# Where the tables of the third and fourth slot and the scale of the second matrix stand in a gated cross-attention kernel

## The chip, the cores and the metric

The kernel runs on one core of a Trainium2 chip. The metric is the device time of one execution in microseconds (us). The engines are TensorE (PE in the profile, with its weight loads as PEld), VectorE (DVE), ScalarE (ACT), GpSimd (POOL) and SyncE (SP). Each works through its own instructions in a fixed order and waits on semaphores for the others.

## The reference

There are 16 sequences, each with 224 tokens of width 512 and a context of 750 rows of width 384, part of them masked. Cut to what matters:

```python
# attention block
q = layernorm(x) @ W_q ; k = context @ W_k ; v = context @ W_v       # 8 heads of 64
attn = softmax(where(mask, q @ k.T / 8, -max))
x = x + tanh(g_xattn) * ((attn @ v) @ W_o + b_o)
# feed-forward block: 512 -> 2048 -> 512, activations and weights quantised
def weight_quant(w):                       # a matrix of -1, 0, 1 times one scale
    scale = 1 / clip(mean(abs(w)), 1e-5)
    return clip(round(w * scale), -1, 1) / scale
h = gelu(act_quant(rmsnorm(layernorm(x))) @ weight_quant(w1).T + b1)
x = x + tanh(g_ffn) * (act_quant(rmsnorm(h)) @ weight_quant(w2).T + b2)
```

The scale of a weight matrix needs the mean over the whole matrix, so no element of it can be rounded before all of it has been summed.

## The kernel before

**Slots.** The mask keeps few context rows of each sequence, so only kept rows are loaded. The sequences are sorted by their number of kept rows; sequence number s of that order is "slot s". Slots 0 to 7 hold up to 192 rows, slots 8 to 15 up to 128. The work of a slot s has these parts, by function of `compact_path`:

- `select(s)` makes the tables. Six VectorE comparisons write `ind` (L830, one buffer for all slots), twelve small matmuls sum it into `pi` (L836), two VectorE instructions turn `pi` into row numbers `keys` (L850), and one writes the mask (L866).
- `gather(s)` (L880) issues two indirect DMAs from GpSimd that fetch the context rows by `keys` into `ctx`, which has two buffers.
- `context_pieces(s)` is a list of pieces: transposes of the context (`ctxp`, L905), keys (`kp`, L916, two pieces) and values (`vp`, L931, and `vr`, L942).
- `query_pieces(s)` transposes normalised tokens (`xnp`, L1014) and makes queries (`qp`, L1035). `norm_pieces(s)` normalises tokens on VectorE and GpSimd (L979 to L988) and fetches later ones (L807).
- `scores(s, n)`, n from 0 to 3, makes a quarter of the slot's scores (`sim`, L1074), takes maxima on VectorE (L1088), exponentials on ScalarE (L1098), the reciprocal of the sums on VectorE (L1107), and scales the probabilities on GpSimd (L1108). `turn_probs` transposes them (`ptp` L1128, `ptr` L1135) and `weighted(s)` multiplies them with the values (`av`, L1151 and L1166).

**Weights.** The two feed-forward matrices are prepared beside slots 0 and 1. `load_weights` brings chunks of [128, 1024] into `raw`, `sum_weights` (L1388 on VectorE, L1392 on ScalarE) sums them, `scale_weights(wi)` (L1398 to L1411) ends in one matmul `wtotp` (L1400) and a few tiny VectorE instructions that make the scale. `round_weights` then needs two VectorE instructions a chunk (L1421 writes integers into `raw`, L1422 clips them into `w16`, which has three buffers), and `turn_weights` transposes a chunk (`wp`, L1441 for the first matrix, L1445 for the second) and evicts it as fp8. There are eight chunks a matrix. A chunk of the second matrix is loaded into the buffer of `raw` that the same chunk of the first has left.

**Order.** Program order is made by `merge`, which interleaves three streams (attention of slot s, `other`: what prepares slot s + 1 and later ones, and `flow`: weights or feed-forward) by the costs written beside the pieces. `weave` mixes the context pieces and the query pieces of the next slot. A scheduler then places the instructions on the engines. Ahead of the loop stands a block under `behind`, with the scores of slot 0, the sums of the first matrix, `scale_weights(0)` and `select(2)`. In the loop, slot s emits `norm_pieces(s + 2)`, `gather(s + 2)`, `select(s + 3)` and then the woven pieces of slot s + 1. In slot 1 `scale_weights(1)` is the first piece of `flow`.

**Pools.** After slot 1 the pool `raw` (eight buffers of 4 KB in a partition) is closed and the pool `rows` (`y`, `hq`, `hqT`, eight buffers of 4 KB) is opened in its place. From then on `residual` fetches tokens into `y` (L807) and adds a bias on GpSimd (L1207); the first three such pairs can be fetched early.

Of the kernel before, what the change touches and what calls it, by code (L numbers as in the profile page):

```python
# [733 lines left out]
def compact_path(ctx, tc, sh, x, context, out, late_loads, stages):  # L734
# [5 lines left out]
    B, S, D = x.shape  # L740
# [82 lines left out]
    def select(s):  # L823

        st = live[s]
        cap = CAPS[s]
        nt = 2 if cap > P else 1
        ind = pa.tile([TJ, NJ, 192], BF16, tag="ind", name=f"ind_{s}", bufs=1)
        for n in range(NJ):
            nc.vector.tensor_scalar(ind[:, n, :cap], sh.place[:TJ, :cap], sh.upto[:, n, s : s + 1], None, ALU.is_ge)  # L830
        load["v"] += 6 * 170
        pi = gen([P, 2], F32, f"pi_{s}")
        for t in range(nt):
            rows = rows_of(s, t)
            for n in range(NJ):
                nc.tensor.matmul(  # L836
                    pi[:rows, t : t + 1],
                    lhsT=ind[:, n, t * P : t * P + rows],
                    rhs=sh.one[:, 0:1],
                    start=(n == 0),  # L840
                    stop=(n == NJ - 1),
                )

        if s > 1:
            keys = pa.tile([P, 2], I32, tag="keys", name=f"keys_{s}", bufs=3)
        else:
            keys = across.tile([P, 2], I32, name=f"keys_{s}")
        for t in range(nt):
            rows = rows_of(s, t)
            nc.vector.tensor_scalar(  # L850
                keys[:rows, t : t + 1],
                pi[:rows, t : t + 1],
                float(J - 1),
                sh.first[:rows, s : s + 1],
                ALU.min,
                ALU.add,
            )
        st["keys"] = keys

        if s > 1:  # L860
            mb = pa.tile([TQ, 320], F32, tag="mask", name=f"mask_{s}", bufs=1)
        else:

            mb = early[:TQ, 2 * RING + 2 * s * S : 2 * RING + 2 * s * S + 320]
        nm = 320 if nt > 1 else P
        nc.vector.tensor_scalar(  # L866
            mb[:, :nm], sh.place_f[:TQ, :nm], sh.slots[:TQ, 0, s : s + 1], -FMAX, ALU.is_ge, ALU.mult
        )
        st["mask"] = mb

    def gather(s):
        st = live[s]
        nt = 2 if CAPS[s] > P else 1
        if s:
            kept = pa.tile([P, 2, C], F32, tag="ctx", name=f"ctx_{s}", bufs=2)
        else:
            kept = early[:, 2 * D : 2 * D + 2 * C].rearrange("p (t c) -> p t c", t=2)
        for t in range(nt):
            rows = rows_of(s, t)
            nc.gpsimd.indirect_dma_start(  # L880
                out=kept[:rows, t, :],
                out_offset=None,
                in_=kctx,
                in_offset=bass.IndirectOffsetOnAxis(ap=st["keys"][:rows, t : t + 1], axis=0),
                bounds_check=B * J - 1,
                oob_is_err=False,
            )
        st["ctx"] = kept
# [137 lines left out]
    def query_pieces(s):  # L1026
        st = live[s]

        def query(p):
            if p == 0:  # L1030
                st["qT"] = pa.tile([P, NP, S], F32, tag="qT", name=f"qT_{s}", bufs=2)
            pq = gen([P, 2, S], F32, f"qp_{s}_{p}")
            for i in range(2):
                for d in range(ND):
                    nc.tensor.matmul(  # L1035
                        pq[:, i, :],
                        lhsT=sh.wq[:, d, (p + i) * P : (p + i + 1) * P],
                        rhs=st["xnT"][:, d, :],
                        start=(d == 0),
                        stop=(d == ND - 1),  # L1040
                    )
            evict(st["qT"][:, p : p + 2, :], pq, 2 * S)

        pieces = [(0.4, lambda t=t: turn(t)) for t in tiles_of(s)]
        pieces += [(3.0, lambda p=p: query(p)) for p in (0, 2)]
        return pieces
# [151 lines left out]
    late = {}  # L1198
# [197 lines left out]
    def scale_weights(wi):  # L1396
        tot = small(f"wtot_{wi}")
        nc.vector.tensor_reduce(tot[:, 0:1], weight_sums[wi], AX.X, ALU.add)  # L1398
        pt = gen([P, 1], F32, f"wtotp_{wi}")
        nc.tensor.matmul(pt, lhsT=sh.ones, rhs=tot[:, 0:1], start=True, stop=True)  # L1400
        mean = small(f"wmean_{wi}")
        nc.vector.tensor_scalar(mean[:, 0:1], pt, 1.0 / (FF * D), 1e-5, ALU.mult, ALU.max)
        sw = pa.tile([P, 1], F32, name=f"sw_{wi}")
        nc.vector.reciprocal(sw, mean[:, 0:1])
        isw = pa.tile([P, 1], F32, name=f"isw_{wi}")
        nc.vector.reciprocal(isw, sw)
        if wi == 0:
            nc.vector.tensor_scalar(isw, isw, 1.0 / 127.0, None, ALU.mult)
        else:

            nc.vector.tensor_scalar(isw, isw, sh.tgates[:, 1:2], 1.0 / 127.0, ALU.mult, ALU.mult)  # L1411
        weight_scale[wi] = sw
        sh.isw[wi] = isw
# [35 lines left out]
    def weight_pieces(wi):  # L1449

        p = []
        if wi == 1:
            p += [(0.0, lambda: scale_weights(1))]
        for c in range(NPC + 2):
            if c < NPC:
                p += [(0.2, lambda c=c: round_behind(wi, c))]
                if wi == 0:
                    p += [(0.0, lambda c=c: load_weights(1, c))]
            if c > 1:
                p += [(0.6, lambda c=c: turn_weights(wi, c - 2))]  # L1460
                if wi == 0:
                    p += [(0.0, lambda c=c: sum_weights(1, c - 2))]
        return p
# [18 lines left out]
    def weave(a, b):  # L1482

        outl = []
        ia = ib = 0
        while ia < len(a) or ib < len(b):
            if ib >= len(b) or (ia < len(a) and ia * len(b) <= ib * len(a)):
                outl.append(a[ia])
                ia += 1
            else:  # L1490
                outl.append(b[ib])
                ib += 1
        return outl
# [30 lines left out]
    with ExitStack() as behind:  # L1524
        for instruction in latest.values():
            behind.enter_context(tc.issue_after(instruction))
        scores(0, 0)
        scores(0, 1)
        for _, piece in queries[3:] + keys_values[3:]:
            piece()  # L1530
        for c in range(NPC):
            sum_weights(0, c)
        for _, piece in norm_pieces(1):
            piece()
        scores(0, 2)
        scores(0, 3)
        scored = latest["max"]
        scale_weights(0)
        select(2)

        held = [sh.wo[0:1, 0, 0:1], sh.wo[0:1, 2, 0:1], sh.wo[P // 2 : P // 2 + 1, 2, 0:1]]
        for dst in held + [sh.bo[0:1, 0:1], sh.b1[0:1, 0:1], sh.b2[0:1, 0:1]]:
            nc.scalar.copy(dst, weight_sums[0][0:1, NPC - 1 : NPC])
# [4 lines left out]
    projected = raised = lowered = 0  # L1548
    for s in range(B):
        other = norm_pieces(s + 2) if s + 2 < B else []  # L1550
        if s + 2 < B:
            other.append((0.0, lambda s=s: gather(s + 2)))
        if s + 3 < B:
            other.append((0.0, lambda s=s: select(s + 3)))
        if s + 1 < B:
            other += weave(context_pieces(s + 1), query_pieces(s + 1))
        flow = []
        if s < 2:
            flow = weight_pieces(s)
        else:  # L1560
            complete = 256 * (projected + 1) <= S * s
            if projected == 0:
                nc.gpsimd.tensor_scalar(sh.bo, sh.bo, sh.tgates[:, 0:1], None, ALU.mult)
                nc.gpsimd.tensor_scalar(sh.b2, sh.b2, sh.tgates[:, 1:2], None, ALU.mult)
            if complete:
                flow.append((0.0, lambda i=projected: residual(i)))
            if raised < projected:
                flow += up_pieces(raised)
                raised += 1
            if complete:  # L1570
                flow += project_pieces(projected)
                projected += 1
                if lowered < raised:
                    flow += down_pieces(lowered)
                    lowered += 1
        merge(attention_pieces(s), other, flow)
        if s == 1:

            late["stage"].close()
            late["rows"] = ctx.enter_context(tc.tile_pool(name="rows", bufs=1))  # L1580
        if s + 1 < B:
            scores(s + 1, 0)
            scores(s + 1, 1)
# [45 lines left out]
```

## Time and profile before

| | |
|---|---|
| median of 3 runs | 754.19 us (750.54 to 754.37) |
| the profiled execution | 754.13 us |
| its span, first to last instruction | 752.3 us |
| mean granted TensorE clock | 0.969 |
| busy: PE, DVE, ACT, POOL | 680.9, 502.4, 408.2, 396.7 us |
| from 37.4 us to 74.8 us (first scores of slot 0's second half to first scores of slot 1) | TensorE idle 3.38, 1.44 and 0.96 us |
| from 74.8 us to 111.0 us (first scores of slot 1 to those of slot 2) | TensorE idle 2.73 and 1.26 us, and 0.16 us |
| from 111 us to 640 us | TensorE idle 10.7 us in nine waits for the scaled probabilities (L1108, the longest 3.4), at most 1.8 us in any other wait |

The busy time of an engine says how loaded it is, and the idle times with what ended them say where another engine sets the pace. Since the loop has one order on every engine, an instruction that comes late on one engine holds back everything behind it there. The two stretches in the table are the ones that the change reorders.

### The profile page before, as it was taken

Reading aid. Unit: us, or ns where it says so; the run is one execution under the profiler, and the core shown is the slowest. Engines: PE = TensorE matmul, PEld = TensorE weight load, DVE = VectorE, ACT = ScalarE, POOL = GpSimd, SP = SyncE. Lnnn points to the kernel's source line nnn. Section 1 sums busy time; section 2 is a strip of 40 time slices with the busy share of each in tenths; the row PEclk is TensorE's granted clock in tenths of the full one; section 3 lists DMA queues with packets and bytes.
Section 4 is the critical chain, followed back from the end, with each engine's and each line's share of the span. In section 5 each row is a group of like instructions: output and inputs, shape, how many; then the busy total and the mean of one; then the engine's idle time right before and its main releaser. Section 6 shows DMA issues by size and latency. Waiting matters only on the chain.

```text
span 752.3 us, 11360 instructions
## 1 busy us (share of the span) xinstructions
PE 680.9 (91%) x3900; PEld 433.7 (58%) x3900; DVE 502.4 (67%) x1284; ACT 408.2 (54%) x963; POOL 396.7 (53%) x541
## 2 busy tenths in 40 slices
PE   4979799999999999998999999999999999889642
PEld 3867677675656565665655665666666656433221
DVE  5595856866684674755749667497675949495860
ACT  2557645383763836635757368274655656560530
POOL 5593675463654645546356564565654544535141
PEclk9989899999999999999999999999999999999877
DMA  7775031032222322122233313132131222223250
GB/s 240 275 240 177 27 88 31 15 73 57 82 51 60 87 57 71 40 71 68 36 91 75 84 53 62 43 89 62 54 74 54 57 71 57 71 52 54 47 102 31
DMA packets 87218, 58.77 MB, mean 78 GB/s; under 512 B 75488, under 2 KB 75632, under 8 KB 87024
## 3 DMA queue, kind: packets, MB, share of 16 engines
q1 hardware_dynamic: 79024, 32.00, 18.7%
q0 software_dynamic: 8128, 25.96, 11.0%
q8 instruction: 33, 0.54, 0.3%
q14 instruction: 33, 0.27, 0.1%
HBM read 32.26 MB, written 7.34 MB: 53 GB/s over the span
## 4 chain that ended last, share of the span: by engine, by line
PE 50%; DVE 17%; issue 12%; POOL 9%; ACT 5%; DMA 5%; POOLq 0%; ACTq 0%; DVEq 0%; SPq 0%
PE qp L1035 9%; PE op L1214 8%; PE fp L1329 8%; PE hp L1284 6%; PE vp L931 4%; PE kp L916 3%; PE sim L1074 3%; DVE a L1307 3%; PE ptp L1128 2%; PE av L1151 2%; DVE h L1292 2%; ACT p L1098 2%; DVE p L1088 2%; DVE hq L1310 2%; POOL p L1108 2%
## 5 line engine op out<-in xcount | busy, mean ns | idle before, releaser
L1329 PE MATMUL fp<-w2T,hqT 128*128 128x512 fp8e4 x448 | 106.7, 394 | 14.9 <-DMA hqT<-hq 14.9
L1108 POOL TENSOR_TENSOR p<-p,rec 112x768 f32<-112x768 f32 (+1 forms) x64 | 83.5, 1307 | 68.0 <-DVE rec L1107 42.8
L1284 PE MATMUL hp<-w1T,xqT 128*128 128x512 fp8e4 x448 | 107.2, 384 | 8.8 <-DVE h L1292 6.1
L1098 ACT ACTIVATE p<-p,nm 112x192 f32<-112x192 f32 (+1 forms) x256 | 106.4, 418 | 11.8 <-DVE nm L1088 11.6
L1035 PE MATMUL qp<-xnT,wq_sb 128*128 128x224 f32 x512 | 105.2, 359 | 0.6 <-ACT xnT L780 0.6
L1214 PE MATMUL op<-wo_sb,xoT 128*128 128x512 f32 x224 | 103.7, 599 | 0.0
L1035 PEld LDWEIGHTS qp<-xnT,wq_sb 128*128 128x128 f32 x512 | 97.1, 193 | 6.4 <-issue 3.3
L1292 DVE SCALAR_TENSOR_TENSOR h<-hp,c,b_bc 128x1024 f32<-128x1024 f32 x56 | 71.6, 1279 | 40.8 <-PE hp L1284 38.3
L1329 PEld LDWEIGHTS <-hqT 128*128 128x128 bf16 x448 | 44.0, 101 | 73.6 <-DMA hqT<-hq 17.5
L1088 DVE CUSTOM_DVE_ANT_0 p<-sim,mask 112x128 f32<-112x128 f32 (+1 forms) x224 | 57.7, 313 | 33.0 <-PE sim L1074 33.0
L1307 DVE TENSOR_REDUCE a<-h 128x1 f32<-128x2048 f32 x28 | 63.9, 2282 | 22.7 <-ACT h L1304 22.6
L1284 PEld LDWEIGHTS <-xqT 128*128 128x128 bf16 x448 | 43.5, 98 | 58.0 <-issue 16.0
L1333 DVE SCALAR_TENSOR_TENSOR y<-fp,c,y 128x512 f32<-128x512 f32 x28 | 20.9, 745 | 81.0 <-PE fp L1329 81.0
L1335 POOL DMA_INDIRECT out_dram<-y,token x28 | 30.8, 1099 | 80.0 <-DVE y L1333 75.7
L1315 ACT ACTIVATE h<-h 128x2048 f32<-128x2048 f32 x28 | 53.4, 1908 | 21.9 <-DVE hq L1310 14.5
L1304 ACT ACTIVATE h<-h 128x2048 f32<-128x2048 f32 x28 | 53.5, 1909 | 18.3 <-DVE k L1225 11.2
L1214 PEld LDWEIGHTS op<-wo_sb,xoT 128*128 128x128 f32 x224 | 40.6, 190 | 38.9 <-issue 36.4
L916 PE MATMUL kp<-ctxT,wk_sb 128*128 128x192 f32 (+1 forms) x384 | 61.2, 307 | 0.0
L916 PEld LDWEIGHTS kp<-ctxT,wk_sb 128*128 128x128 f32 x384 | 55.7, 194 | 6.2 <-issue 4.3
L1272 POOL TENSOR_TENSOR y<-y,b_bc 128x512 f32<-128x512 f32 x28 | 36.5, 1304 | 39.0 <-DVE fx L1253 38.7
L780 ACT COPY pT<-ptp 128x448 f32<-128x448 f32 x62 | 32.2, 536 | 39.7 <-PE ptp L1128 38.7
L1074 PE MATMUL sim<-kT,qT 64*112 64x192 f32 (+1 forms) x512 | 49.8, 313 | 0.3 <-DVE h L1292 0.2
(173 smaller groups left out, 1182.3 us busy)
## 6 DMA issues: line engine op xcount, KB each, us to landing
raw<-in_L_ffn_w_dram SPq DMA_DIRECT2D x16, 512.0 KB
wq_sb<-in_L_xattn_W_q_dram SPq DMA_DIRECT2D x1, 1024.0 KB
b_bc<-in_L_ffn_b_dram SPq DMA_DIRECT2D x1, 1024.0 KB
wk_sb<-in_L_xattn_W_k_dram SPq DMA_DIRECT2D x1, 768.0 KB
wv_sb<-in_L_xattn_W_v_dram SPq DMA_DIRECT2D x1, 768.0 KB
wo_sb<-in_L_xattn_W_o_dram SPq DMA_DIRECT2D x1, 512.0 KB
wo_sb<-in_L_xattn_W_o_dram SPq DMA_DIRECT2D x2, 256.0 KB
y<-in_x_dram,token POOLq DMA_INDIRECT x28
```

The source lines that it names most:

```text
L916: nc.tensor.matmul(pk[:, p - p0, :], lhsT=sh.wk[:, c, p * P : (p + 1) * P], rhs=st["ctxT"][:, c, :cap], start=(c == 0), stop=(c == NC - 1),)
L1035: nc.tensor.matmul(pq[:, i, :], lhsT=sh.wq[:, d, (p + i) * P : (p + i + 1) * P], rhs=st["xnT"][:, d, :], start=(d == 0), stop=(d == ND - 1),)
L1074: nc.tensor.matmul(sim[:, j, i, :cap], lhsT=st["qT"][j * DH : (j + 1) * DH, p, q * TQ : (q + 1) * TQ], rhs=st["kT"][j * DH : (j + 1) * DH, ...
L1088: latest["max"] = nc.vector.tensor_tensor_reduce(out=probs[:, h, :cap], in0=sim[:, j, i, :cap], in1=st["mask"][:, j * begin : j * begin + ...
L1098: nc.scalar.activation(probs[:, h, :cap], probs[:, h, :cap], AF.Exp, bias=nmax, scale=-1.0, accum_out=total[:TQ, h : h + 1],)
L1108: nc.gpsimd.tensor_tensor(probs[:, :, :cap], probs[:, :, :cap], rec[:TQ].unsqueeze(2).to_broadcast([TQ, 4, cap]), ALU.mult,)
L1214: nc.tensor.matmul(po, lhsT=xoT[:, d, at : at + P], rhs=sh.wo[:, d, :], start=(d == 0), stop=(d == ND - 1))
L1284: nc.tensor.matmul(ph[:, n, :], lhsT=f["xqT"][:, k * ND + d, :], rhs=w1T[:, d, at : at + NB], start=(d == 0), stop=(d == ND - 1),)
L1292: nc.vector.scalar_tensor_tensor(h[:, cols], ph.rearrange("t i n -> t (i n)"), f["c1", k], sh.b1[:, cols], ALU.mult, ALU.add)
L1304: nc.scalar.activation(f["h", k], f["h", k], AF.Gelu)
L1307: nc.vector.tensor_reduce(amax[:, k : k + 1], h, AX.X, ALU.max, apply_absolute_value=True)
L1329: nc.tensor.matmul(po, lhsT=f["hqT", k][:, n, :], rhs=w2T[:, n, :], start=(n == 0), stop=(n == NF - 1))
```

## The change

`select(2)` leaves the block ahead of the loop. In slot 0 the first five pieces of the woven list for slot 1 (`of_next`: transposes of context and tokens, the first keys piece) now come before `select(2)` and `gather(2)`, and `select(3)` comes after all of that list. In later slots nothing is reordered in `other`. In `flow` of slot 1, an empty piece of cost 3.0 stands ahead of `scale_weights(1)`, so that `merge` emits other work first. The pool `rows` is opened with `reuse_waits="tile"`: each of its tiles waits for the users of the part of the old pool that it covers, and no longer for all users of the old pool.

```diff
@@ weight_pieces(wi)
         if wi == 1:
-            p += [(0.0, lambda: scale_weights(1))]
+            p += [(3.0, lambda: None), (0.0, lambda: scale_weights(1))]
@@ block ahead of the loop
         scored = latest["max"]
         scale_weights(0)
-        select(2)
@@ the loop over slots
         other = norm_pieces(s + 2) if s + 2 < B else []
-        if s + 2 < B:
+        of_next = weave(context_pieces(s + 1), query_pieces(s + 1)) if s + 1 < B else []
+        if s == 0:
+
+            other += of_next[:5] + [(0.0, lambda: select(2)), (0.0, lambda: gather(2))]
+            of_next = of_next[5:] + [(0.0, lambda: select(3))]
+        elif s + 2 < B:
             other.append((0.0, lambda s=s: gather(s + 2)))
-        if s + 3 < B:
-            other.append((0.0, lambda s=s: select(s + 3)))
-        if s + 1 < B:
-            other += weave(context_pieces(s + 1), query_pieces(s + 1))
+            if s + 3 < B:
+                other.append((0.0, lambda s=s: select(s + 3)))
+        other += of_next
@@ after slot 1
             late["stage"].close()
-            late["rows"] = ctx.enter_context(tc.tile_pool(name="rows", bufs=1))
+            late["rows"] = ctx.enter_context(tc.tile_pool(name="rows", bufs=1, reuse_waits="tile"))
```

## Prediction

> **What bounds the kernel now.** I read the page's busy table first, then its slices, then the waits of TensorE in the early stretch, then the chain there, then the granted clock in windows.
>
> ```profile
> PE 680.9 (91%) x3900; PEld 433.7 (58%) x3900; DVE 502.4 (67%) x1284; ACT 408.2 (54%) x963; POOL 396.7 (53%) x541
> PE   4979799999999999998999999999999999889642
> ```
>
> TensorE is busy 91% of the span. In slices of 18.8 us it is at 9 from the eighth slice until near the end; the holes are before 112 us and in the tail. The tail's order is the same before and after, so only the early holes matter. The waits between 36 and 112 us name them (engine, what waited, releaser: total, times, longest):
>
> ```profile
> PE pi L836 <- DVE isw L1408: 3.4, 1, 3.4
> PE wtotp L1400 <- DVE wtot L1398: 2.7, 1, 2.7
> PE wp L1441 <- DVE w L1422: 1.4, 1, 1.4
> PE wp L1445 <- DVE w L1422: 1.3, 1, 1.3
> PE wp L1441 <- ACT qT L780: 1.0, 1, 1.0
> ```
>
> That is 9.8 us of idle TensorE. The first wait is for the table `ind` of slot 3, which VectorE writes just behind that `isw`. The chain of waits (start, length, what) shows the table work ahead of the first rounding:
>
> ```profile
> 42.82 0.17 DVE ind L830
> ...
> 43.05 1.41 DVE ind L830 x5
> 44.45 1.87 DVE raw L1421
> ...
> 46.76 0.60 DVE w L1422
> ```
>
> The idle time has a second price. Here are windows of 3.41 us: stretch, length, busy time of PE, PEld, DVE, ACT, POOL, then the granted clock, DMA share and GB/s.
>
> ```profile
> 77.91:81.32 3.41, 1.42 (x15) 0.81 (x11) 3.26 (x18) 3.09 (x15) 1.47 (x1) 1.00 0.01 2
> 81.32:84.73 3.41, 1.51 (x6) 1.14 (x6) 2.95 (x18) 1.59 (x7) 3.12 (x4) 0.50 0.00 0
> 84.73:88.15 3.42, 3.20 (x17) 2.87 (x18) 3.42 (x6) 1.80 (x5) 3.31 (x3) 0.50 0.00 0
> 40.36:43.77 3.41, 0.73 (x5) 0.50 (x5) 3.41 (x25) 3.41 (x16) 2.63 (x2) 1.00 1.12 262
> 43.77:47.19 3.42, 2.22 (x17) 1.56 (x15) 3.42 (x10) 1.22 (x4) 3.25 (x3) 0.50 0.50 201
> 47.19:50.60 3.41, 3.18 (x17) 2.84 (x18) 3.41 (x7) 1.79 (x4) 3.41 (x1) 0.50 0.53 173
> 60.84:64.25 3.41, 2.44 (x19) 1.65 (x18) 2.83 (x6) 3.41 (x8) 2.76 (x3) 1.00 0.52 160
> ```
>
> A window with 0.73 or 1.42 us of TensorE work is followed by two at half clock; one with 2.44 us is not. The two half-clock spells hold 5.4 and 4.7 us of work, so they cost about 2.7 and 2.35 us. Idle and clock together: some 15 us, the most this change could touch.
>
> [...] both spells last 6.83 us, two such windows, and a window need not be wholly idle (1.42 us busy sufficed). [...] the rounding L1422 has a median of 682 ns, and one beginning at 95.01 us took 2.90 while GpSimd ran two L1108 from 94.46 to 97.35. [...] The gather at 45.94 us took 5.41 us against 0.95 for an undisturbed one.
>
> **The change, slot 0.** The order of the built programs shows: the tables of slot 2 (six L830, one L866) move ahead of everything, to 17 us, where VectorE waits 9.21 us, so they cost nothing; without that cover they would cost 1.3 us. `pi` and `keys` of slot 2 go behind the second `ptr` of slot 0; all of `select(3)` goes behind the roundings and to the end of slot 0.
>
> Until 40 us little moves: 0.15 + 0.15 + 0.74 + 0.29 us of tables leave, but the scheduler puts two more statistics (L979, 1.2 us) there, so the maxima of the second half start at 39.75 instead of 40.01. After them, 0.23 (keys) + 0.17 + 1.41 us of tables and 0.1 of gaps go, so the first L1421 can start at 42.4 instead of 44.45. [...] Bounds for the end of `w16` 0: 44.7 (VectorE always first) and 47.7 (GpSimd always between); before, 47.36. I take 46.0, so `wp` 0 starts 1.3 us earlier than 47.42.
>
> TensorE meanwhile does `ctxp` and `xnp` at 39.2 to 41.1 and then stands idle for 5 us, so the first half-clock spell stays[...]; half of the 1.3 us is lost to it. Against it, both `pi` groups (0.52 us each), earlier in idle time, now stand on the busy stretch: +1.0. The wait of 0.96 for ScalarE, whose sum was held by the DMA of a `raw` chunk, should go, since the buffer comes free about 2 us sooner. Sum: -1.3 + 0.65 + 1.0 - 0.96 = -0.6 us at slot 1's first scores (bounds -1.2 and +0.3).
>
> The gathers: GpSimd no longer has gather(2) (5.41 + 0.96 us) ahead of the L1108 of the fourth quarter. gather(2), now waiting for `keys` 2 at about 52 us, lands by 60 and is needed at 75; gather(3) at 75, needed at 112. Queued behind the latter is the first L1108 of slot 1, 3.7 us later than `keys` 3; two gathers of 1.0 to 1.3 us fit. SP's queue keeps its order.
>
> **Slot 1.** Let S be the start of its first scores (74.81 before). Before, `wp` 0 of the second matrix started at S + 10.14 and the first scores of slot 2 at S + 36.18. After, `wtotp` stands behind all keys pieces, so TensorE does 6.9 us more ahead of `wp` 0 (xnp 0.44, ctxp 0.35, kp 4.1, ptp and ptr 1.2, av 0.83). Walking the new orders with the durations of this trace:
>
> - The tables of slot 4 (five L830, 0.85 us) now stand between `keys` 3 and the maxima: first maximum at S + 1.25 instead of S + 0.89.
> - The second keys half waits for `ctxT`, behind ScalarE's exponentials (S + 6.5): 0.4 us idle.
> - On GpSimd a gather of slot 4 and a token fetch (1.0 us each, 0.3 between) stand ahead of the second L1108, and the six L830 of slot 5, blocked by the first L1108 until S + 5.2, ahead of its reciprocal: L1108 ends at S + 9.7, TensorE was there at 8.5: 1.2 us idle.
> - TensorE ends `av` at S + 14.05. VectorE makes the scale at S + 14.2, behind four maxima that needed the late sixteenth of the scores. L1421 and L1422 (1.25 us) compete with GpSimd's normalisation (to S + 14.9) and an L1108. `w16` 0 between S + 15.6 and, with both L1108 let in, S + 18.6; I take 16.4: idle 2.3 us.
>
> From there 17.2 us of TensorE work (qp 6.2, vp 2.6, wp 3.6, ptp and ptr 1.2, av 0.83 + 0.92, vr 1.45, and 0.5 of waits on evictions) lead to slot 2. S + 33.6 without a half-clock spell: 2.6 us gained. [...] a spell of 3.4 to 5 us then costs some 2 us. Weighted: -1.3 us (bounds: -3.4, and +2.2 with S + 18.7 and a spell of 2.5).
>
> `reuse_waits` lets GpSimd fetch `y` before the last rounding (99.6 us) has passed. [...] VectorE is then through at about S + 33.2, needed at S + 32 to 33: +0.3 us (0 to 1.7). From slot 2 on the orders agree but for one scores matmul, and the gain passes through.
>
> Sum: -0.6 - 1.3 + 0.3 = -1.6; 754.13 - 1.6 = **752.5 us**, as good as the median (754.19).
>
> **Rivals.** *The likeliest* (0.43) is this: idle is moved rather than removed, 752.5 (750.5 to 757.8). *Faster* (0.41): [...] slot 1 loses its half-clock spell: -1.2 - 3.4 = -4.6, about 749.5. For it: at 83.4 to 86.2 us VectorE ran undisturbed against small GpSimd operations, and one of the three runs before was 3.7 us shorter. Against: the 2.90 above. *Slower* (0.16): [...] Both L1108 get in ahead of `w16` 0 in slot 1 (S + 18.7, spell 2.5: +2.2), the adds hold the last `wp` 1.7 us, and slot 0 loses 0.3: +4.2, 758.3. It decides from `w16` 0 at about S + 17 on, where the old order's extra work is used up. *No effect at all*: the built orders differ on four engines, so only a cancellation could look like that; it is in the likeliest.
>
> **The numbers.** 0.5% is 3.8 us, about what a measurement of this kernel can tell from no change (its three runs span that). Range 747 to 758: the faster case but for its tail, the likeliest whole; about 2 in 10 lie outside.
>
> **What would show it.** Right: the wait of `wtotp` gone; a TensorE idle of about 5 us before the first `wp` L1441 and about 2.3 before the first `wp` L1445; a new wait of `ptp` for L1108 in slot 1; half clock near 44 to 51 us. Wrong: `w16` 0 of the second matrix before S + 15 or after S + 18, waits over 2 us in the last `wp`, or a slot 2 whose distance to the end differs by over 1 us from before.

## The result and the profile after

The changed kernel takes 756.98 us in the median (22 runs, 753.4 to 762.2) against 754.38 us (22 runs) for the kernel before: a ratio of 1.0038, 95% interval 1.0022 to 1.0055. It is 2.6 us slower, where 1.6 us faster was forecast. The profiled execution took 758.43 us, its span is 756.7 us, its mean granted clock 0.967; the two profiled executions differ by 4.4 us in their spans, which is more than the medians do.

The page, busy table (engine, busy us, share, instructions) and TensorE's slices, of the kernel after:

```profile
PE 686.0 (91%) x3900; PEld 435.8 (58%) x3900; DVE 500.4 (66%) x1284; ACT 408.0 (54%) x963; POOL 390.8 (52%) x541
PE   4969799999999999998999999999999999879652
```

TensorE is busy 5.1 us longer with the same 3900 instructions, so part of the loss is slower work and not waiting. The three longest waits of TensorE from 30 to 125 us of the kernel after (total, times, longest):

```profile
PE wp L1441 <- DVE w L1422: 5.9, 1, 5.9
PE wp L1445 <- DVE w L1422: 4.3, 1, 4.3
PE pi L836 <- DVE ind L830: 0.5, 1, 0.5
```

The two waits for `isw` (3.4) and `wtot` (2.7) are gone, and the two for the first rounded chunk of each matrix (`w16` 0) have taken up all of it: the idle time was moved into two long pieces. What held the one in slot 1 stands in the timelines of VectorE and GpSimd of the kernel after (start, length, what):

```profile
90.47 0.17 DVE L1406 RECIPROCAL isw<-sw 128x1 f32<-128x1 f32 x1
90.55 2.87 DVE L1421 TENSOR_SCALAR raw<-raw,sw 128x1024 int32<-128x1024 f32 x1
93.34 0.20 DVE L1411 TENSOR_SCALAR isw<-isw,tgates 128x1 f32<-128x1 f32 x1
93.47 0.68 DVE L1422 TENSOR_SCALAR w<-raw 128x1024 bf16<-128x1024 int32 x1
...
88.49 1.52 POOL L988 TENSOR_SCALAR x<-x,ls_x,rs_x 128x512 f32<-128x512 f32 x2
89.99 2.88 POOL L1108 TENSOR_TENSOR p<-p,rec 112x768 f32<-112x768 f32 x2
```

The first L1421 of the second matrix begins 0.56 us behind the start of two back-to-back L1108 and ends 0.55 us behind their end: 2.87 us instead of 0.7. And in windows of 3.41 us (stretch, length, PE, PEld, DVE, ACT, POOL, clock, DMA share, GB/s), what the wait brings:

```profile
89.44:92.85 3.41, 0.49 (x6) 0.09 (x2) 3.28 (x7) 0.00 (x0) 3.41 (x3) 1.00 0.03 8
92.85:96.27 3.42, 2.06 (x12) 1.96 (x13) 3.42 (x7) 0.99 (x1) 1.56 (x3) 0.50 0.00 0
96.27:99.68 3.41, 3.41 (x11) 3.09 (x10) 2.61 (x4) 0.02 (x1) 0.86 (x1) 0.50 0.51 154
```

A window with 0.49 us of TensorE work is followed by two at half clock, and in TensorE's timeline the queries lie in them:

```profile
95.03 5.54 PE L1035 MATMUL qp<-xnT,wq_sb 128*128 128x224 f32 x16
...
107.05 3.25 PE L1035 MATMUL qp<-xnT,wq_sb 128*128 128x224 f32 x16
```

The same sixteen matmuls take 5.54 us there and 3.25 us a little later. **In slices of the loop:** from slot 1's first scores (S, at 74.74 and 75.31 us in these timelines) to the first `op` (L1214) the kernel before takes 39.11 us and the kernel after 42.23, which is 3.1 of the 4.4 us between the two spans. Another 0.6 us was there before 37 us; it does not follow the change, since a kernel with the moved tables (`e3` below) lacks it and one without them (`e9`) has most of it. Slot 0 is even within 0.1, and 0.7 lies behind the first `op`.

The 3.1 us of slot 1 are not all waiting. Here is the stretch from S to behind the first scores of slot 2 (columns as above), and in it the scores matmuls (busy us, mean ns of one, idle before), the kernel before first each time:

```profile
74.81:112.41 37.60, 33.33 (x271) 26.92 (x270) 25.93 (x77) 21.02 (x57) 27.24 (x24) 0.91 0.20 58
75.31:116.11 40.80, 35.85 (x273) 27.79 (x271) 26.65 (x85) 21.14 (x57) 24.71 (x24) 0.92 0.22 60
L1074 PE MATMUL sim<-kT,qT 64*112 64x192 f32 x48 | 5.0, 337 | 0.1
L1074 PE MATMUL sim<-kT,qT 64*112 64x192 f32 x48 | 6.5, 346 | 0.0
```

TensorE's idle time grew by 0.7 us there and its busy time by 2.5, at nearly the same mean clock. So both kernels have a half-clock spell of two windows in slot 1, and the one of the kernel after lies on denser work (5.5 us of busy time in it, 4.7 before). The pause also changes how `merge` mixes the streams: the 48 scores matmuls, which stood in blocks of sixteen, stand for the greater part in pieces of 2 to 12 among other work, and TensorE is busy with them for longer. What makes the pieces longer no run tests.

### The profile page after: what moved, and what is told of

Same layout as the page of the kernel before. It is cut to its first block, busy times and chain, and to the rows that moved or that the text cites. A ratio compares the mean times of both kernels' runs of the same rounds, so it can differ in the third digit from the quotient of the medians.

```text
span 756.7 us, 11352 instructions
## 1 busy us (share of the span) xinstructions
PE 686.0 (91%) x3900; PEld 435.8 (58%) x3900; DVE 500.4 (66%) x1284; ACT 408.0 (54%) x963; POOL 390.8 (52%) x541
## 3 DMA queue, kind: packets, MB, share of 16 engines
q1 hardware_dynamic: 79024, 32.00, 18.8%
## 4 chain that ended last, share of the span: by engine, by line
PE 47%; DVE 16%; issue 14%; POOL 13%; ACT 5%; DMA 4%; POOLq 0%; ACTq 0%; SPq 0%; DVEq 0%
PE qp L1035 8%; PE fp L1329 8%; PE op L1214 7%; PE hp L1284 6%; PE kp L916 4%; DVE a L1307 3%; PE vp L931 3%; PE sim L1074 3%; POOL p L1108 3%; DVE h L1292 2%; PE ptp L1128 2%; PE av L1151 2%; DVE hq L1310 2%; POOL y L807 2%; DMA hqT<-hq 2%
## 5 line engine op out<-in xcount | busy, mean ns | idle before, releaser
L1329 PE MATMUL fp<-w2T,hqT 128*128 128x512 fp8e4 x448 | 108.6, 399 | 13.0 <-DMA hqT<-hq 13.0
L1108 POOL TENSOR_TENSOR p<-p,rec 112x768 f32<-112x768 f32 (+1 forms) x64 | 84.3, 1320 | 54.4 <-DVE rec L1107 30.1
L1035 PE MATMUL qp<-xnT,wq_sb 128*128 128x224 f32 x512 | 108.3, 367 | 0.6 <-ACT xnT L780 0.6
L1214 PE MATMUL op<-wo_sb,xoT 128*128 128x512 f32 x224 | 103.8, 600 | 0.0
L1035 PEld LDWEIGHTS qp<-xnT,wq_sb 128*128 128x128 f32 x512 | 99.6, 199 | 7.2 <-issue 3.3
L1088 DVE CUSTOM_DVE_ANT_0 p<-sim,mask 112x128 f32<-112x128 f32 (+1 forms) x224 | 57.8, 313 | 34.6 <-PE sim L1074 34.5
L1315 ACT ACTIVATE h<-h 128x2048 f32<-128x2048 f32 x28 | 53.4, 1907 | 22.0 <-DVE hq L1310 14.6
L1304 ACT ACTIVATE h<-h 128x2048 f32<-128x2048 f32 x28 | 53.5, 1909 | 18.7 <-DVE k L1225 11.6
L1214 PEld LDWEIGHTS op<-wo_sb,xoT 128*128 128x128 f32 x224 | 40.7, 190 | 38.8 <-issue 36.3
L1272 POOL TENSOR_TENSOR y<-y,b_bc 128x512 f32<-128x512 f32 x28 | 36.5, 1305 | 39.1 <-DVE fx L1253 38.8
L780 ACT COPY pT<-ptp 128x448 f32<-128x448 f32 x62 | 32.2, 537 | 39.8 <-PE ptp L1128 38.5
L780 ACT COPY qT<-qp 128x448 f32<-128x448 f32 x30 | 15.9, 531 | 68.5 <-PE qp L1035 68.3
```

Source lines behind the costliest of these rows:

```text
L1035: nc.tensor.matmul(pq[:, i, :], lhsT=sh.wq[:, d, (p + i) * P : (p + i + 1) * P], rhs=st["xnT"][:, d, :], start=(d == 0), stop=(d == ND - 1),)
L1088: latest["max"] = nc.vector.tensor_tensor_reduce(out=probs[:, h, :cap], in0=sim[:, j, i, :cap], in1=st["mask"][:, j * begin : j * begin + ...
L1108: nc.gpsimd.tensor_tensor(probs[:, :, :cap], probs[:, :, :cap], rec[:TQ].unsqueeze(2).to_broadcast([TQ, 4, cap]), ALU.mult,)
L1214: nc.tensor.matmul(po, lhsT=xoT[:, d, at : at + P], rhs=sh.wo[:, d, :], start=(d == 0), stop=(d == ND - 1))
L1304: nc.scalar.activation(f["h", k], f["h", k], AF.Gelu)
L1315: nc.scalar.activation(f["h", k], f["h", k], AF.Square, accum_out=ss[:, k : k + 1])
```

## The experiments

**Theory.** The pause (the empty piece of cost 3.0) ahead of `scale_weights(1)` loses the time: it puts the first rounding of slot 1 under two L1108 of GpSimd, and the long wait of TensorE brings half clock over the queries. **Rivals:** the moved tables and gathers, or `reuse_waits`, lose it; or the wait is set by `wtotp`, not by the two L1108 of GpSimd. All ratios are to the kernel before in the same comparison, with a 95% interval.

**One edit alone, and one edit less.** The edits are three. Five runs and the kernels before and after make seven of their eight combinations.

`e1_pause_only`, the kernel before with

```diff
-            p += [(0.0, lambda: scale_weights(1))]
+            p += [(3.0, lambda: None), (0.0, lambda: scale_weights(1))]
```

> The kernel before with one edit of the four: the empty piece of cost 3.0 ahead of scale_weights(1). Theory (the late scale of the second matrix meets GpSimd's two L1108 of slot 1, and the half-clock spell that follows falls on the queries): all of the loss is here, 757 to 758 us, with a TensorE idle of over 3.5 us before the first wp of the second matrix and an L1421 of over 2 us. Rival (the moved tables and gathers cost the time): as before, 754.4. Rival (reuse_waits): as before, 754.4.

Measured: 762.78 us (6 runs), 1.0113 (1.0077 to 1.0149). The loss is there and larger than forecast, but not by the way of the theory: in the profile the first L1421 of the second matrix takes 1.13 us, and the idle before its `wp` is 2.35 us. TensorE waits earlier, for an L1108, and the second keys piece takes 4.21 us, by that length at half clock (2.22 us elsewhere):

```profile
85.57 0.60 PE L1128 MATMUL ptp<-ident,p 112*128 112x112 f32 x4 [2.06 <-POOL p L1108]
88.44 4.21 PE L916 MATMUL kp<-ctxT,wk_sb 128*128 128x192 f32 x12
```

`wtotp` behind it comes at S + 17.3 instead of S + 13.4, and the first `wp` at S + 21.1. So the theory's way is that of the kernels that also have the move (after, and `e5` below with an L1421 of 2.88 us).

`e2_no_pause`, the kernel after with that line undone.

> The kernel after without the empty piece: the moved tables and gathers and reuse_waits stay. Theory: slot 1 has its scale early again, the first L1421 takes 0.7 us, 753 to 754.5 us. Rival (moved tables and gathers) and rival (reuse_waits): 756.5 to 757.5, no nearer to before than the whole change.

Measured: 752.07 us, 0.9964 (0.9942 to 0.9986), a little below the forecast.

`e5_no_tile`, the kernel after with the pool opened as before:

```diff
-            late["rows"] = ctx.enter_context(tc.tile_pool(name="rows", bufs=1, reuse_waits="tile"))
+            late["rows"] = ctx.enter_context(tc.tile_pool(name="rows", bufs=1))
```

> The kernel after with the pool rows opened as before, without reuse_waits; the order on every engine stays as in the kernel after. Theory (reuse_waits is not part of the loss; the y fetches waited for the last rounding in the profile after, and the adds met none): 757 us, within 0.5 of the kernel after. Rival (the early fetches cost time): 755.5 or less.

Measured: 760.24 us (6 runs), 1.0110 (1.0070 to 1.0150). The expectation was wrong, and so was my reading of `reuse_waits`: without it the change loses about three times as much (758.5 to 767.6 us, so the size is rough).

`e6_move_only`, both lines undone, and `e9_tile_only`, the kernel before with `reuse_waits` alone.

> The kernel before with only the move of the tables and gathers of the third and fourth slot (the kernel after without the empty piece and without reuse_waits). Theory (the move alone carries the gain of 2.3 us that the kernel without the empty piece showed): 751.5 to 752.5 us. Rival (the gain came from reuse_waits): 754 us.

Measured: 753.06 us, 0.9995 (0.9970 to 1.0020).

> The kernel before with only reuse_waits on the pool rows; the order on every engine stays that of the kernel before. Theory (the two early y fetches shorten GpSimd's chain to the first L1108 of slot 2 by up to 2.6 us, of which the kernel before can use less than 2, since its last rounding comes early): 752 to 753.8 us. Rival (reuse_waits brings nothing where the pause is missing, and the gain of the kernel without the empty piece needs the move as well): 754.2.

Measured: 754.18 us, 1.0016 (0.9996 to 1.0035).

What follows, dividing ratios of kernels that differ in one edit:

| edit | beside | ratio | us |
|---|---|---|---|
| pause | move and reuse_waits (after / e2) | 1.0074 ± 0.0028 | +5.6 |
| pause | move (e5 / e6) | 1.0115 ± 0.0047 | +8.7 |
| pause | nothing (e1) | 1.0113 ± 0.0036 | +8.5 |
| move | nothing (e6) | 0.9995 ± 0.0025 | -0.4 |
| move | pause (e5 / e1) | 0.9997 ± 0.0054 | -0.2 |
| reuse_waits | move and pause (after / e5) | 0.9929 ± 0.0043 | -5.4 |
| reuse_waits | move (e2 / e6) | 0.9969 ± 0.0033 | -2.3 |
| reuse_waits | nothing (e9) | 1.0016 ± 0.0020 | +1.2 |

The pause is the only loss. The profiles agree: from S to the first `op` the three kernels with the pause and no remedy (after, `e1`, `e5`) take 42.2 to 43.5 us, and the four without it (before, `e2`, `e6`, `e9`) 39.1 to 39.8. The move of the tables and gathers does nothing that can be measured. `reuse_waits` gives back over half of what the pause costs; away from the pause its two values differ in sign and the intervals of both hold no change, so only the case with the pause is settled. The gain of `e2` over the kernel before is found in neither of its two edits alone (`e6`, `e9`); where it comes from stays open.

Why it matters there, in the waits of TensorE from 100 to 300 us, `e5_no_tile` first and the kernel after second:

```profile
PE ptp L1128 <- POOL p L1108: 5.7, 3, 3.2
```

```profile
PE ptp L1128 <- POOL p L1108: 2.5, 2, 1.3
```

and in GpSimd's timeline, again `e5_no_tile` and then the kernel after:

```profile
105.89 1.09 POOL L807 DMA_INDIRECT y<-in_x_dram,token  x1 [15.61 <-DVE w L1422]
...
122.05 2.89 POOL L1108 TENSOR_TENSOR p<-p,rec 112x768 f32<-112x768 f32 x2
```

```profile
94.42 1.35 POOL L807 DMA_INDIRECT y<-in_x_dram,token  x1 [1.55 <-DVE w L1422]
96.07 1.05 POOL L807 DMA_INDIRECT y<-in_x_dram,token  x1 [0.30 <-issue]
107.77 1.20 POOL L807 DMA_INDIRECT y<-in_x_dram,token  x1 [10.64 <-DVE w L1422]
...
121.44 2.89 POOL L1108 TENSOR_TENSOR p<-p,rec 112x768 f32<-112x768 f32 x2
```

The `y` fetches and their adds stand in GpSimd's queue ahead of the first L1108 of slot 2. Without `reuse_waits` all of them wait for the last rounding, and the L1108 comes 16.2 us after that; with it the first two fetches go early and it comes 13.7 us after. TensorE waits 3.2 us less, which is the part of the 5.4 us that the traces show; the interval (2.1 to 8.6) holds it. The pause makes the last rounding late (the fetch starts at S + 25.1 in the kernel before and at S + 33.2 in `e5`), so this chain becomes the bound in slot 2 when the pause is there: `e1` has the long wait too (3.3 us), and the four kernels without the pause have none above 1.5 us between 100 and 300 us.

**What the pause costs in slot 1.** `e3_no_lock`, the kernel after with

```diff
-        nc.gpsimd.tensor_tensor(
+        if s != 1 or n < 2:
+            nc.gpsimd.tensor_tensor(
...
```

> The kernel after with the two GpSimd instructions L1108 of slot 1's third and fourth quarter left out (these probabilities stay unscaled); no order on the other engines changes. Theory: the first L1421 of the second matrix takes 0.7 instead of 2.9 us, the idle before its wp falls from 4.3 to about 2.2 us, and the time falls by 2 us, or by up to 4.5 if the half-clock spell goes with it: 752.5 to 755. Rival (the wait is set by the late wtotp matmul itself[...]): the idle stays above 3.5 us and the time at 756.5 to 757.5.

Measured: 753.68 us, 0.9993 (0.9975 to 1.0011), 3.4 us below the kernel after. The first rounding in VectorE's timeline of `e3_no_lock` (its lines stand one further down: L1422 here is L1421 of the kernel after), and TensorE's wait behind it:

```profile
89.17 0.73 DVE L1422 TENSOR_SCALAR raw<-raw,sw 128x1024 int32<-128x1024 f32 x1
```

```profile
90.69 0.62 PE L1446 MATMUL wp<-ident,w 128*128 128x128 bf16 x8 [2.14 <-DVE w L1423]
```

0.73 us instead of 2.87, an idle of 2.14 instead of 4.28, and the first `wp` at S + 16.8 instead of S + 18.9. VectorE's order is that of the kernel after, so GpSimd alone made the difference. The rival (`wtotp`) falls for half of the wait; the 2.14 us that stay are the way from `wtotp` over the scale to `w16` 0. Beside the two L1108, which ran for 2.88 us in a row in the kernel after, the L1421 took 2.14 us more than here. What in the two instructions kept VectorE from going on the traces do not show.

`e4_fill` and `e7_fill_short`, the kernel after with five and with three matmuls in the wait:

```diff
         pt = gen([P, 8, P], BF16, f"wp_{wi}_{c}")
+        if wi == 1 and c == 0:
+            keep = pt.rearrange("p a b -> p (a b)").bitcast(F32)
+            first = nc.tensor.matmul(keep[:, 0:1], lhsT=ident, rhs=late["mean"][:, 0:1], ...).ins
+            with tc.issue_after(first):
+                for k in range(3):        # 5 in e4_fill
+                    nc.tensor.matmul(keep, lhsT=ident, rhs=sh.wq[:, 0, :512], ...)
```

> The kernel after with five idle-filling matmuls of 128x512 (0.61 us each, 3.0 us in all, results overwritten) in the wait before the first wp of the second matrix; the wait itself stays. Theory (half of the loss is the clock): qp behind it takes 3.3 instead of 5.5 us, wp 0.6 instead of 1.0, the half-clock spell of slot 1 is gone, 754 to 754.7 us. Rival (only the wait counts, clock windows cost little as in the kernel before): 756 to 757.

Measured: 758.76 us, 1.0060 (1.0041 to 1.0079). The fills were sized wrongly: 0.61 us was the length of one record, and a 128x512 product has two of them here, 0.9 us. The five took 4.54 us in the profiled execution, and the first `wp` came 0.75 us after `w16` 0 was ready, so they made the wait longer. The queries behind it took 3.25 us, by that length at full clock. But that execution (755.05 us) is the second fastest of 22 and does not explain the median, which lies above that of the kernel after. Why it does stays open, and the run settles nothing on the clock's price.

> The kernel after with three instead of five idle-filling matmuls of 128x512 (0.91 us each by the run with five, so 2.7 us in a wait of 4.3), so that they end ahead of the data they wait with. Theory (the half-clock spell behind the long wait costs 2 to 2.7 us in the executions that have it): 754.5 to 755.5 us. Rival (the spell is not set by this wait): 757 us, with the mean clock at 0.967 as in the kernel after.

Measured: 753.19 us, 0.9990 (0.9963 to 1.0017), 3.6 us (give or take 2.4) below the kernel after; the median of the mean clocks is 0.974, against 0.968. TensorE's timeline of `e7_fill_short` (L1452 is its `wp` of the second matrix):

```profile
93.61 0.62 PE L1452 MATMUL wp<-ident,w 128*128 128x128 bf16 x8 [0.84 <-DVE w L1423]
94.06 3.25 PE L1035 MATMUL qp<-xnT,wq_sb 128*128 128x224 f32 x16
```

The L1421 still takes 2.86 us and the first `wp` still comes at S + 18.9; only the clock is kept up (granted 1.00 from 88.5 to 96.0 us), and the queries take 3.25 us. From S to the first `op` it is 39.57 us, against 42.23: of the 3.1 us of slot 1, 2.7 go with the spell. This does not mean that the kernel before has no spell; it has one on lighter work. TensorE's busy time in that stretch, without the 3.2 us of the fill and its gate, is 34.5 us in `e7` (at full clock by the lengths of its instructions) and 34.8 in the kernel before at a mean clock of 0.91, so the new order's work is the longer one at equal clock, by some 2 us (an estimate, with the 2.35 us that the prediction counted for the old spell). `e3` and `e7` bring back the same microseconds in two ways (their sum, 7.0, is more than the pause costs, so they share a part). In the profiled execution of `e3` the spell was still there by the length of the queries (4.93 us for 3.25).

**Attempts at a better version**, all on `e2_no_pause`, which beats both kernels, except `e11`. `e8_pin_first` puts the first L1422 of slot 0 ahead of the second L1421:

```diff
-            with tc.issue_after(scored):
+            with tc.issue_after(late["clipped"] if c else scored):
                 round_weights(wi, c)
```

> The kernel after without the empty piece, and with the clip L1422 of the first chunk of the first matrix placed directly behind its L1421, ahead of the second chunk's L1421 (1.0 us in the profile after). Theory (the first wp L1441 waits for exactly these instructions): the idle before it is 1 us shorter and the time 751 us, 1 below the kernel without the empty piece. Rival [...]: no gain, 752.

Measured: 753.31 us, 0.9978 (0.9962 to 0.9994). In its profile L1421 and L1422 took 1.18 and 0.97 us, and the idle before the first `wp` was 4.1 us (4.7 without the pin). 0.6 us are gained there and not seen in the whole; no better than `e2`.

`e10_fill0` has three such filling matmuls in slot 0's wait, and `e11_fill_both` is the kernel after with three in each slot's.

> The kernel after without the empty piece, with three idle-filling matmuls of 128x512 (2.7 us, gated by wmean of the first matrix, results overwritten) in the wait ahead of the first wp L1441 of slot 0. Theory (the half-clock spell of slot 0 costs 2.1 us by the lines behind it: kp 3.29 for 2.22, xnp 1.11 for 0.66, wp 1.03 for 0.61, ctxp 0.72 for 0.5): 749.5 to 750.5 us, 2 below the kernel without the empty piece. Rival (the spell falls on transposes that are slow anyway): 752.

Measured: 752.80 us, 0.9999 (0.9977 to 1.0021). In the profiled execution the fills stand behind an idle of 1.63 us and by their length themselves met the half clock: they took 4.52 us instead of 2.8, and the first `wp` came at 46.22 us, though its `w16` was ready at 44.2. There the spell was shifted onto the fills, not removed. That execution has a lower mean clock (0.968) than most of the others (median 0.972, against 0.969 for `e2`), so the clock did rise and still no time was gained; why stays open.

> The whole change with three idle-filling matmuls in each of the two long waits, ahead of the first wp L1441 of slot 0 and ahead of the first wp L1445 of slot 1. Theory (both half-clock spells are set by those waits): 2 below the kernel with the fill of slot 1 alone, 751 to 752 us, mean clock 0.973 or more. Rival (only slot 1's spell costs): 753 to 753.5 us.

Measured: 756.24 us (6 runs), 1.0055 (1.0034 to 1.0077). Both waits were filled in the profiled execution, and the clock fell elsewhere, in slot 1's keys (see below). Why this is slower than `e7` in the median stays open.

`e12_early_scale` goes the other way than the pause. Beside these lines `scale_weights(1)` is taken out of `weight_pieces`:

```diff
+        if s == 0:
+            scale_weights(1)
         if s + 1 < B:
             scores(s + 1, 0)
```

> The opposite of the empty piece: the kernel after with scale_weights(1) emitted ahead of slot 1's first scores (and without the empty piece), so that the scale is made right behind the last sum of the second matrix and the first L1421 stands among the maxima of slot 1. Theory (the place of the scale sets how long TensorE waits in slot 1): the waits for wtotp (2.5 us) and for the first wp L1445 (1.4 us) shrink to under 1.5 us together, the half-clock spell of slot 1 goes in most executions, 749 to 751 us. Rival (VectorE's maxima come later instead and TensorE waits for the probabilities, or the roundings meet GpSimd's L1108 of the first half): 752 to 754.

Measured: 753.32 us, 0.9987 (0.9963 to 1.0010). In its profile the two waits fell to 0.94 us together, but an L1421 met an L1108 again (1.96 us), the half clock was there for about one window (0.93 and 0.57 in two of 3.41 us), and TensorE waited 1.8 us for a later L1108. From S to the first `op` it is 38.0 us, the least of all profiles. In the whole, no gain that can be told from none. With `e2` at 0.9964, `e8` at 0.9978, `e10` at 0.9999 and this one, the kernel without the pause is the best seen, by 0.36% (0.14 to 0.58); how much of that would stay is not settled.

## Why the prediction was wrong

**The failed step is the first rounding of slot 1.** The prediction put `w16` 0 of the second matrix at S + 16.4 between bounds of 15.6 and 18.6, the latter "with both L1108 let in". It came at S + 18.8: both were let in, whole. The prediction had the price in the trace of before (an L1422 of 2.90 us beside two L1108, for 0.68) and chose a value near the bound without it. In `e3`, without the two L1108, `w16` 0 is ready at S + 16.7. So 2.1 us of the 3.2 above the free bound are the two L1108. The other 1.1 are mostly the scale, forecast at S + 14.2 and made at S + 15.1: in both kernels the evictions of the second keys piece (0.56 and 0.43 us) stood ahead of it on VectorE, where the prediction had four maxima. That `e3` is so near to 16.4 is luck.

**The idle** was then 4.28 us and not 2.3.

**The half-clock spell** was counted at 2 us with a weight of two thirds, 1.3 us; the weight was my estimate, and no trace shows it. The idle of 4.28 us left 0.49 us of work in a window of 3.41 us; in the trace of before one with 1.42 us was followed by half clock. The spell lay on the queries: 2.3 us there and 0.4 in the first `wp`. That is 2.7. In the kernel before the spell lay on transposes, half a set of keys and two of the waits. Wait (+2.4) and spell (+1.4) make 3.8 of the 4.4 us by which slot 1 missed (-1.3 forecast, +3.1 in the trace). Another 0.5 is the work behind the wait: at full clock, in `e7`, it takes 20.7 us from the first `wp` to the first `op`, where the forecast leads to 20.1 (17.2 to the first scores of slot 2, and 2.9 from there in the kernel before).

**The adds of `reuse_waits`** were put at +0.3 us, on my estimate that six L1207 would hold up the last roundings. They met none: the second pair of fetches waited 10.64 us for the last rounding. What the step left out is GpSimd's own queue, in which fetches and adds stand ahead of slot 2's first L1108. The late last rounding holds that queue, and `reuse_waits` frees a part of it, worth -5.4 us beside the pause. The prediction counted neither, and in slot 2 of the kernel after the two about cancel. That is luck: `e5` shows the first without the second.

**The waits for `ctxT` and L1108 in slot 1** (0.4 and 1.2 us) did not come in the kernel after; a wait of 0.5 us for `ind` did. TensorE still ended `av` at S + 14.6, later than the forecast of 14.05, so its own work ahead of the wait was put too low. The one for L1108 is in `e1`, with 2.06 us, and keys at half clock behind it (4.21 us for 2.22).

**Slot 0.** The first `wp` came 0.85 us earlier, by the distance to the last scores (9.21 for 10.06 us), with 1.3 forecast: a second L1421 of 1.02 us and an L1422 of 1.94 us beside an L1108 stood before it. The wait for ScalarE went, as forecast. The spell stayed, but 1.3 us later (45.06 to 51.89 us), so that the first keys took 3.29 us for 2.50. In this pair of executions S moved by less than 0.1 us, not by 0.6. One pair settles little: with the new order in slot 0 seven profiles (after, `e2` to `e7`) have 36.0 to 37.4 us from the last scores of slot 0 to S, 36.9 in the mean, and with the old order three (before, `e1`, `e9`) have 37.1 to 37.4, mean 37.2.

**The slower rival** named what happened, with S + 18.7 and a spell of 2.5 us. Its other two terms (the adds, a loss in slot 0) did not come, and slot 1 cost 3.1 us in the traces where it had 2.2. **From slot 2 on** the distance to the end was to agree within 1 us, and it did (638.5 and 639.2 us from the first `op`).

## What to carry to other kernels

A producer that is moved later must be checked against what the other engines do at the new place (here an L1421 took 2.87 us beside two L1108 and 0.73 us without them); where two bounds differ by such a stop, price both, and do not take a value near the free one. A wait of TensorE can cost its length and the clock of the work behind it (here 4.28 us, and 2.7 us more in the work behind), so filling a wait that can't be removed may be worth as much as removing it (`e7` lies 3.6 us below the kernel after; `e3`, where the wait is half as long, 3.4), if the fill is shorter than the wait and starts at once; of four kernels with fills here, one was faster than the same kernel without. Buffers that come free late can hold a queue, and what counts is everything behind the waiting instruction there (the L1108 came 16.2 us behind the last rounding in `e5`, 13.7 in the kernel after).

## What the runs showed that was not expected

**Most of the scatter is the clock.** In one comparison a run of the kernel before took 750.2 us at a mean clock of 0.974 and another 760.8 at 0.958. One spell of two windows is 6.83 us at half clock, 0.0045 of the mean. Over the 51 executions of the kernel before in that comparison, 0.001 of mean clock goes with 0.67 us (correlation -0.93), so a spell goes with some 3 us (an estimate from these two). One spell more or less weighs as much as this whole change.

**Half clock also came behind a busy window.** In `e11_fill_both` three windows at half clock followed one in which TensorE was busy for 2.90 of 3.41 us (windows as above):

```profile
75.09:78.50 3.41, 2.90 (x30) 1.99 (x26) 3.27 (x23) 2.81 (x12) 1.99 (x3) 1.00 0.29 89
78.50:81.91 3.41, 3.41 (x11) 2.24 (x10) 2.09 (x9) 2.52 (x10) 2.94 (x4) 0.50 0.17 46
```

That window holds the one-column matmuls `pi` and a wait of 0.5 us. It is one execution. In the trace of before, half clock followed windows with 0.73 and 1.42 us of work and not one with 2.44; so busy time by the records does not tell which window it follows. What does was not tried.
